# A fused attention and convolution network in fp32: one weight sum per attention block, adding transfers for three of fifteen additions, and compact divisions

## The chip, the cores and the metric

The kernel runs on one core of one Trainium2 chip. The metric is device time in microseconds (us) of one execution. The kernel before took 2679.58 us, the median of three runs (2674.23 to 2680.1). The profile comes from one further execution.

The core has five engines, each with a queue of its own that is worked off in order: TensorE (PE) for matmuls, VectorE (DVE) for elementwise work and reductions, ScalarE (ACT) for activation functions and copies, GpSimd (POOL), and SyncE (SP), which here issues the DMAs. Matmuls write PSUM, which has eight banks of 512 fp32 columns; everything else lives in SBUF.

## The reference

The input is 16 frames of 384 channels and 16 x 16 points, in two batches of 2048 tokens each. Four layers follow each other; all numbers are fp32. The change is in layer 0, attention in 12 heads of 32 channels, whose values are the input itself:

```python
xt = x.reshape(B, NUM_FRAMES, C, H, W).transpose(0, 2, 1, 3, 4)
xt = xt.reshape(B, C, N).transpose(0, 2, 1)
qk = (xt @ qk_w.T).reshape(B, N, 2, nh, HEAD_DIM)
...
attn = jax.nn.softmax(jnp.einsum('bhnd,bhmd->bhnm', q * scale, k), axis=-1)
...
attn = alpha * eye + beta * attn - gamma * Cm
out = jnp.einsum('bhnm,bhmd->bhnd', attn, v)
```

Layer 1 is a 7 x 7 depthwise convolution, a layer norm, a two-matrix MLP with a gelu and a response norm, and a residual. Layer 2 is two Sobel edge maps, a fusion matmul, a layer norm, a gelu and a residual. Layer 3 is two pointwise convolutions with a 3 x 3 depthwise one between them, linear attention, and a second MLP.

## The kernel before, in words

**Blocks.** A batch is cut into four blocks of 512 tokens (`BLK`), so there are eight blocks in the layers behind attention. In attention a *unit* is one batch and one group of four heads (six units); a unit has four blocks of 512 queries, so there are 24 attention *blocks*, and each has 16 *steps* `t`, one for every 128 keys.

**One step.** `scores` runs four matmuls of 32 rows, one for each head, into two double-bank PSUM tiles `st`, and two exps of 128 x 1024 into two SBUF tiles `e` (L461 to L479). The loop (L585 to L595) emits the scores of step t+1 before the `weighted` of step t. `weighted` (L481) runs four matmuls of 32 columns that add the four heads' weighted values into one bank `av`, and then VectorE adds the exps into running sums `s`, two additions of 128 x 1024. An fp32 matmul is recorded as two instructions, so four heads show as eight.

**Weight sums.** The softmax's denominators are sums of the exps over the keys. VectorE adds up `adds` steps' exps elementwise, and TensorE then sums over the 128 partitions by a matmul with ones into the bank `dn` (`weights`, L524). `ADDS` (L55) holds for each of the 24 blocks how many steps go into one sum: 16, 8, 4 or 2. All but a block's last sum are cut into four quarters of 128 columns that are spread over later steps (L505 to L512).

**End of a block.** `finish` (L536) copies `dn` to `r` with a row total for the safety test, and puts four reciprocals of 128 x 128, a scaling of `va` by `r`, the output `put` and a second total `check` into `due`, a table of what is to be emitted at which later step. `va` and `xg` (L516 to L521) are ScalarE's copy of `av` and the part with alpha and gamma.

**Projections.** In step 5 (`SLOT`) of most blocks two projections of the next queries or keys run, three matmuls of 128 x 512 each (L592).

**Filling.** `fill` (L1481) uses VectorE's free time in attention for layer 1's convolutions of the first two blocks (`YB`), written as `y`, and for the first steps of layer 1 itself (the `leads`: a centring with a matmul `su`, a variance with a matmul `sv`, a square root, a reciprocal). `pace` (L194) holds the time that the planner expects of each step on TensorE and VectorE. PSUM in attention is three double tiles for scores and projections, and one bank each for `av` and `dn` (L412, L413).

**Behind attention** everything is written as tasks of operations with costs, and `Plan.all` (L180) emits them in an order that it works out from those costs, from `RANK` and `SLACK`. `TURNS` (L36) is the order in which blocks pass through the two MLPs; at every turn the MLP's weights are loaded anew, three times 768 KB for each of two matrices.

`InOrder` (L96) records every operation, so nearly all rows of the profile have this line and are told apart by their tiles.

Of the kernel before, what the change touches and what calls it, by code (L numbers as in the profile page):

```python
# [13 lines left out]
PSUM = bass.MemoryType.PSUM  # L14

P = 128
# [15 lines left out]
SLOT = 5  # L32
LEAD = 20 * NQC + 6
# [4 lines left out]
    (1, ((0, 0), (0, 1),)),  # L38
    (0, ((1, 0), (1, 2),)),
    (1, ((0, 2),)),  # L40
    (0, ((1, 1), (1, 3),)),
    (1, ((1, 0), (0, 3), (1, 2), (1, 1), (1, 3),)),
)
AFTER = ('x4', 0, 2)

RANK = {
    "mid": ((36.6, 22.0, 24.3, 85.6), (18.6, 42.9, 96.6, 26.9)),
    "l1": ((50.1, 89.5, 75.2, 4.0), (51.1, 16.8, 81.7, 28.5)),
    "l3c": ((45.7, 99.2, 100.9, 121.0), (-20.9, -6.3, 70.9, 62.0)),
    "conv": 109.4,  # L50
}
SLACK = 0.196
JUNK = 2

ADDS = (16, 8, 16, 16, 4, 4, 4, 2, 2, 8, 16, 16, 4, 16, 2, 4, 16, 8, 4, 4, 4, 4, 4, 4)  # L55
# [61 lines left out]
class Plan:  # L117
# [24 lines left out]
    def run(self, op):  # L142
        at = self.start(op)
        assert at is not None
        for tag, n in op.takes:
            del self.room[tag][:n]
        if op.engine == "PE" and at - self.free_at["PE"] > 2:
            at += 1.5
        if op.engine:
            self.free_at[op.engine] = at + op.length  # L150
        op.ready = at + op.length + op.lag
        for tag, n in op.gives:
            self.room[tag] = sorted(self.room[tag] + [op.ready] * n)
        if op.makes:
            self.made[op.makes] = op
        self.table = op.table or self.table
# [37 lines left out]
def pace(t):  # L194


    n, i = divmod(t - 1, NQC)
    adds = ADDS[n]
    pe, dve = 2.066, 2.275 if t and i % adds else 0.0
    at = i - adds - 1  # L200
    parts = sum(j * adds // 4 == at % adds for j in range(4)) if at >= 0 else 0
    if parts:
        pe += 0.22 * parts
    elif i == 1 and n > 0:
        pe += 0.87
    else:
        pe += 0.09
    if n > 0:
        dve += {2: 0.88, 3: 0.88, 4: 0.88, 5: 0.88, 6: 0.6, 7: 0.66}.get(i, 0.0)
    return pe, dve  # L210
# [187 lines left out]
def attention(tc, X, xt, L0, block, small, col, cols, ones, load_qk, banks, fill, bound):  # L398
# [6 lines left out]
    with ExitStack() as actx:  # L405
# [3 lines left out]
        ep = pool("ep", 8)  # L409
        sp = pool("sp", 4)  # L410
        op = pool("op", 2)
        pst = pool("pst", 3, space=PSUM)  # L412
        pacc = pool("pacc", 1, space=PSUM)  # L413

        def bank2(name):
            return pst.tile([P, 2, BLK], F32, tag="st", name=name)

        banks.append(lambda name: bank2(name)[:, 0, :])
# [35 lines left out]
        due = {}  # L454

        def unit(u, made, gm):
# [3 lines left out]
            adds = ADDS[u * NBLK : (u + 1) * NBLK]  # L460
            acc, sums = {}, {}  # L461

            def scores(n, t):
                es = []
                for i in range(2):
                    es.append(ep.tile([P, 2, BLK], F32, tag="e", name=f"e_{u}_{n}_{t}_{i}"))
                sts = [bank2(f"st_{u}_{n}_{t}_{i}") for i in range(2)]
                for h in range(4):
                    rows = slice(HD * h, HD * (h + 1))
                    pe.matmul(  # L470
                        sts[h // 2][:, h % 2, :],
                        keys[t // TB][rows, ts(t % TB, P)],
                        q[n][rows, :],
                        start=True,
                        stop=True,
                    )
                for i in range(2):
                    act.activation(es[i], sts[i], AF.Exp, scale=HD**-0.5)
                return es  # L479

            def weighted(n, t, es):  # L481
                if t == 0:
                    acc["av"] = pacc.tile([P, BLK], F32, tag="av", name=f"av_{u}_{n}")
                for h in range(4):
                    pe.matmul(
                        acc["av"][HD * h : HD * (h + 1), :],
                        v[t // TB][:, (t % TB) * P + HD * h : (t % TB) * P + HD * (h + 1)],
                        es[h // 2][:, h % 2, :],
                        start=(t == 0),
                        stop=(t == NQC - 1),  # L490
                    )
                at = t % adds[n]
                for i in range(2):
                    if at == 0:
                        sums[i] = es[i]
                    elif at == 1:
                        s = sp.tile([P, 2, BLK], F32, tag="s", name=f"s_{u}_{n}_{t}_{i}")
                        dve.tensor_tensor(s, sums[i], es[i], ALU.add)
                        sums[i] = s
                    else:  # L500
                        dve.tensor_tensor(sums[i], sums[i], es[i], ALU.add)


                k = (u * NBLK + n) * NQC + t
                if at == adds[n] - 1:  # L505
                    parts = 1 if t == NQC - 1 else 4
                    for i in range(parts):
                        due.setdefault(k + 2 + i * adds[n] // 4, []).append(
                            lambda i=i, summed=dict(sums): weights(
                                n, t, summed, ts(i, BLK // parts)  # L510
                            )
                        )  # L512
                for f in due.pop(k, ()):
                    f()
                if t == NQC - 1:
                    va = op.tile([P, BLK], F32, tag="va", name=f"va_{u}_{n}")  # L516
                    act.activation(va, acc["av"], AF.Copy, scale=1.0)
                    xg = op.tile([P, BLK], F32, tag="xg", name=f"xg_{u}_{n}")
                    act.activation(
                        xg, X[b][n][:, g, :], AF.Identity, scale=col("alpha", g), bias=gm  # L520
                    )  # L521
                    due[k + 2].append(lambda: finish(n, va, xg))

            def weights(n, t, summed, at):  # L524
                if t == adds[n] - 1 and at.start == 0:
                    acc["dn"] = pacc.tile([P, BLK], F32, tag="dn", name=f"dn_{u}_{n}")
                for h in range(4):
                    pe.matmul(
                        acc["dn"][HD * h : HD * (h + 1), at],
                        ones[:, :HD],  # L530
                        summed[h // 2][:, h % 2, at],
                        start=(t == adds[n] - 1 and at.start == 0),
                        stop=(t == NQC - 1),
                    )

            def finish(n, va, xg):  # L536
# [4 lines left out]
                r = op.tile([P, BLK], F32, tag="r", name=f"r_{u}_{n}")  # L541
                act.activation(r, acc["dn"], AF.Identity, accum_out=bound[:, 0, k : k + 1])

                def invert(i):
                    dve.reciprocal(r[:, ts(i, P)], r[:, ts(i, P)])
# [3 lines left out]

                def check():  # L550
                    junk = op.tile([P, BLK], F32, tag="junk", name=f"junk_{u}_{n}", bufs=1)
                    act.activation(junk, r, AF.Identity, accum_out=bound[:, 1, k : k + 1])
# [6 lines left out]
                todo = [*(lambda i=i: invert(i) for i in range(TB)), scale, put]  # L559
                for i, f in [*enumerate(todo), (8, check)]:  # L560
                    due.setdefault((k + 1) * NQC + 2 + i, []).append(f)
# [7 lines left out]
        def project(name, steps):  # L569
            pp = bank2(name)  # L570
            for copy in [f(pp[:, i, :]) for i, f in enumerate(steps)]:
                copy()
            return 2.7 * len(steps)
# [5 lines left out]
        for u, (b, g) in enumerate(units):  # L579
# [5 lines left out]
            for n in range(NBLK):  # L585
                for t in range(NQC):
# [5 lines left out]
                    if t == SLOT and steps:  # L592
                        added = project(f"p_{u}_{n}", steps[:2])
                        del steps[:2]
# [10 lines left out]
def conv_seq_kernel(  # L605
# [381 lines left out]
    def second(hid, first, name, ready, last, before=None):  # L987

        po = []
        for f in range(NFC):  # L990
# [6 lines left out]
                gives=[("s", 1)] + ([("wb", 1)] if last and f % NG == NG - 1 else []),  # L997
# [14 lines left out]
    def layer1(b, i):  # L1012
# [8 lines left out]
        gx = pools["tiny"].tile([P, 2, NFC], F32, tag="gx", name=f"gx_{n}")  # L1021
# [56 lines left out]
        po, m = yield from second(hid, at, n, None, last, normed)  # L1078
# [342 lines left out]
    def layer3c(b, i):  # L1421
# [11 lines left out]
        po, m = yield from second(hid, at, n, made, last)  # L1433
# [41 lines left out]
    if fast:  # L1475
# [5 lines left out]
        def fill(t, added=0.0):  # L1481
# [3 lines left out]
            if t < 0:  # L1485
                while plan.step(bias):
                    pass
                return
            if t % NQC == 9 and t > NQC:
# [4 lines left out]
            for task in (*leads, conv):  # L1494
                if task.rest > t or t < (FIRST if task is conv else LEAD):
                    continue
                before = None
                while task is not conv or ("y", 0, YB - 1, NC - 1) not in plan.made:
                    op = task.head
                    if before and before.engine != op.engine:  # L1500
                        task.rest = t + 1 + (before.engine == "DVE")
                        break
                    if op.engine == "DVE":
                        if free < max(0.4, op.length - 1.5):
                            break
# [146 lines left out]
```

## Time and profile before

| | |
|---|---|
| runs shown | 2674.23, 2680.1, 2679.58 us; median 2679.58 |
| the profiled execution | 2679.38 us, span 2677.6 us, mean granted TensorE clock 0.996 |
| PE busy | 2644.6 us (99%), 12997 matmul instructions |
| DVE busy | 2011.5 us (75%) |
| ACT busy | 1557.5 us (58%) |
| POOL busy | 7.4 us |
| DMA | 55.69 MB, 21 GB/s in the mean |
| exps (ACT) | 768 of 128 x 1024, 1025 ns each |
| additions of exps (DVE) | 606 of 128 x 1024, 1216 to 1221 ns each |
| weight sums (PE) | 2016 instructions |
| reciprocals of r (DVE) | 96 of 128 x 128, 939 ns each |

The span is the time between the first and the last instruction; the 1.8 us that the execution took longer lie around it. Attention's first scores start at 22.07 us and layer 1's first MLP matmul at 1052.3 us, so there are three stages: a start, attention, and the rest.

How to read the rows: a row of the timeline gives the start in us, the length in us of all its merged instructions, the engine, the line, the operation, out<-in by the tiles' names, the shape, how many were merged, and in brackets the idle time of the engine before it and what ended that. A row of groups gives busy us and mean ns of one, then idle time before them. A matmul's end is modelled, so for TensorE the distances between starts are the better measure. A duration on ScalarE or VectorE overlaps a little with the next one on that engine. A row of DMA issues gives how many, KB each, and the median us from issue to landing.

### The profile page before, as it was taken

Reading aid. Unit: us, or ns where it says so; the run is one execution under the profiler, and the core shown is the slowest. Engines: PE = TensorE matmul, PEld = TensorE weight load, DVE = VectorE, ACT = ScalarE, POOL = GpSimd, SP = SyncE. Lnnn points to the kernel's source line nnn. Section 1 sums busy time; section 2 is a strip of 40 time slices with the busy share of each in tenths; the row PEclk is TensorE's granted clock in tenths of the full one; section 3 lists DMA queues with packets and bytes.
Section 4 is the critical chain, followed back from the end, with each engine's and each line's share of the span. In section 5 each row is a group of like instructions: output and inputs, shape, how many; then the busy total and the mean of one; then the engine's idle time right before and its main releaser. Section 6 shows DMA issues by size and latency. Waiting matters only on the chain. (4 is left out here: it accounts for less than half of the span.)

```text
span 2677.6 us, 32803 instructions
## 1 busy us (share of the span) xinstructions
PE 2644.6 (99%) x12997; PEld 1061.5 (40%) x12997; DVE 2011.5 (75%) x2588; ACT 1557.5 (58%) x2314; POOL 7.4 (0%) x54
## 2 busy tenths in 40 slices
PE   8999999999999999899999999999999999999999
PEld 2223333233323323345444454444444444454443
DVE  5999999999999889999999999999652202732300
ACT  6787878878787888564565335457443542625201
POOL 0000000000000000000000000000000000000000
PEclk9999999999999999999999999999999999999999
DMA  3000000000000003000001001011001110000000
GB/s 150 5 13 1 9 9 5 13 1 5 13 1 1 1 13 108 23 0 0 1 1 47 25 12 31 29 36 36 24 24 36 47 36 24 0 1 1 12 17 20
DMA packets 28851, 55.69 MB, mean 21 GB/s; under 512 B 1680, under 2 KB 14096, under 8 KB 28688
## 3 DMA queue, kind: packets, MB, share of 16 engines
q1 hardware_dynamic: 28544, 53.35, 6.0%
q8 instruction: 104, 1.70, 0.3%
q14 instruction: 59, 0.48, 0.1%
q10 hardware_dynamic: 144, 0.15, 0.0%
HBM read 47.21 MB, written 6.29 MB: 20 GB/s over the span
## 5 line engine op out<-in xcount | busy, mean ns | idle before, releaser
L96 ACT ACTIVATE e<-st 128x1024 f32<-128x1024 f32 x768 | 743.2, 1025 | 88.5 <-PE st L96 80.7
L96 DVE SCALAR_TENSOR_TENSOR y<-l,vec,y 128x420 f32<-128x420 f32 (+8 forms) x1152 | 660.0, 638 | 5.0
L96 DVE TENSOR_TENSOR s<-s,e 128x1024 f32<-128x1024 f32 x444 | 513.3, 1216 | 11.7 <-ACT e L96 11.2
L96 PE MATMUL st<-q,k 32*128 32x512 f32 x3072 | 474.1, 641 | 4.0 <-ACT e L96 2.3
L96 PE MATMUL av<-e,v 128*32 128x512 f32 x3072 | 410.9, 606 | 4.3 <-ACT va L96 4.2
L96 PE MATMUL ph_l<-y,wa 128*128 128x512 f32 x576 | 261.4, 597 | 0.0
L96 PE MATMUL ph_l3c<-d_l3c,wa 128*128 128x512 f32 x576 | 258.4, 593 | 0.0
L96 PE MATMUL po_l<-hid_l,wb 128*128 128x512 f32 x576 | 255.7, 596 | 1.1 <-ACT hid_l L96 1.1
L96 PE MATMUL po_l3c<-hid_l3c,wb 128*128 128x512 f32 x576 | 256.6, 593 | 0.0
L96 PEld LDWEIGHTS st<-q,k 32*128 32x128 f32 x3072 | 146.1, 183 | 220.1 <-issue 132.4
L96 DVE TENSOR_TENSOR s<-e,e 128x1024 f32<-128x1024 f32 x162 | 191.0, 1221 | 54.7 <-ACT e L96 36.0
L96 ACT ACTIVATE hid_l<-ph_l,vec 128x512 f32<-128x512 f32 x96 | 66.0, 687 | 202.9 <-PE ph_l L96 202.8
L96 ACT ACTIVATE hid_l3c<-ph_l3c,vec 128x512 f32<-128x512 f32 x96 | 65.6, 687 | 202.6 <-PE ph_l3c L96 202.5
L96 PEld LDWEIGHTS av<-e,v 128*32 128x32 f32 x3072 | 60.6, 108 | 298.1 <-issue 274.0
L96 DVE SCALAR_TENSOR_TENSOR o_l3c<-po_l3c,vec,l 128x512 f32<-128x512 f32 x24 | 17.5, 748 | 209.6 <-PE po_l3c L96 208.8
L96 PEld LDWEIGHTS po_l<-hid_l,wb 128*128 128x128 f32 x576 | 109.5, 191 | 139.1 <-issue 128.0
L96 PEld LDWEIGHTS ph_l3c<-d_l3c,wa 128*128 128x128 f32 x576 | 108.8, 190 | 137.2 <-issue 133.4
L96 PEld LDWEIGHTS ph_l<-y,wa 128*128 128x128 f32 x576 | 109.1, 191 | 136.0 <-issue 125.1
L96 PEld LDWEIGHTS po_l3c<-hid_l3c,wb 128*128 128x128 f32 x576 | 109.0, 190 | 134.6 <-issue 132.8
L96 PE MATMUL p<-x,wqk_sb 128*128 128x512 f32 x288 | 132.3, 610 | 1.2 <-DMA x<-in_x_dram 1.2
L96 DVE SCALAR_TENSOR_TENSOR g_l3a<-h_l3a,dw,g_l3a 128x450 f32<-128x450 f32 (+1 forms) x192 | 119.0, 702 | 4.2 <-ACT g_l3a L96 4.1
L96 PEld LDWEIGHTS dn<-s,ones 128*32 128x32 f32 x2016 | 64.1, 110 | 125.4 <-issue 107.0
(155 smaller groups left out, 2446.3 us busy)
## 6 DMA issues: line engine op xcount, KB each, us to landing
wa<-in_w_dram SPq DMA_DIRECT2D x9, 768.0 KB, 4.5
wb<-in_w_dram SPq DMA_DIRECT2D x9, 768.0 KB, 5.0
wa<-in_mlp_w_dram SPq DMA_DIRECT2D x9, 768.0 KB, 4.4
wb<-in_mlp_w_dram SPq DMA_DIRECT2D x9, 768.0 KB, 4.5
x<-in_x_dram SPq DMA_DIRECT2D x8, 768.0 KB, 10.6
v<-in_xt_dram SPq DMA_DIRECT2D x24, 256.0 KB, 2.7
out_dram<-o_l3c SPq DMA_DIRECT2D x24, 256.0 KB, 2.1
qkv<-in_qkv_wT_dram SPq DMA_DIRECT2D x3, 576.0 KB, 11.1
```

The lines of the kernel that those rows point to most:

```text
L96: self.last = self.tc.keep_in_program_order(make(*args, **kw))
```

## The change

It touches attention, and the planner around it.

- **Exps.** A step's four heads get one SBUF tile `e` of 4 x 512 (six of them, in place of eight of 2 x 512 and four sums). PSUM is eight single banks, shared by scores, `av`, `dn` and projections; each head has a bank and an exp of 128 x 512 of its own.
- **Additions.** Each block has one weight sum of all 16 steps. The exps of step 2 are the accumulator. Steps 0, 5 and 10 (`MERGED`) receive the exps of the step behind them by a DMA that adds within SBUF, issued by GpSimd, and VectorE adds the three merged tiles at steps 6, 11 and at the block's end; nine more steps are added by VectorE directly.
- **Weight sum.** Four matmuls with ones once a block, emitted behind the next block's first step and its projections (in the last three blocks three steps later).
- **Divisions.** The denominators of a head stand in 32 equal rows. One row for each head goes to DRAM, comes back as 128 x 16, is inverted there, goes to DRAM again, and comes back spread over 32 rows, by seven DMAs on SP.
- **Projections** move from step 5 to step 0.
- **Filling.** Operations of the leads that switch ScalarE's tables are emitted only at a block's start. `LEAD` lets the first lead in from step 294 and the second not within attention. `pace` has new numbers.
- **Behind attention** `TURNS` has eight turns in place of six, and `RANK`, `SLACK` and `AFTER` have new values; `spent` gives a weight buffer back when the last block of a turn has used it; `gx` has four buffers.

```diff
-ADDS = (16, 8, 16, 16, 4, 4, 4, 2, 2, 8, 16, 16, 4, 16, 2, 4, 16, 8, 4, 4, 4, 4, 4, 4)
+MERGED = {0: 6, 5: 11, 10: NQC}
+PAIRED = (NB * NC - 1) * NBLK + 1
+LEAD = (18 * NQC + 6, 24 * NQC)
...
-    (1, ((0, 0), (0, 1),)),
-    (0, ((1, 0), (1, 2),)),
-    (1, ((0, 2),)),
-    (0, ((1, 1), (1, 3),)),
-    (1, ((1, 0), (0, 3), (1, 2), (1, 1), (1, 3),)),
+    (1, ((0, 0),)),
+    (0, ((1, 0),)),
+    (1, ((0, 1),)),
+    (0, ((1, 2),)),
+    (1, ((1, 0),)),
+    (0, ((1, 3), (1, 1),)),
+    (1, ((0, 2), (0, 3), (1, 2), (1, 1), (1, 3),)),
...
-        ep = pool("ep", 8)
-        sp = pool("sp", 4)
+        ep = pool("ep", 6)
         op = pool("op", 2)
-        pst = pool("pst", 3, space=PSUM)
-        pacc = pool("pacc", 1, space=PSUM)
+        pb = pool("pb", 8, space=PSUM, reuse_waits="tile")
+        dp = pool("dp", 2, space=DRAM)
...
-                for i in range(2):
-                    act.activation(es[i], sts[i], AF.Exp, scale=HD**-0.5)
+                for h in range(4):
+                    act.activation(es[:, h, :], sts[h], AF.Exp, scale=HD**-0.5)
...
+                if t in MERGED:
+                    acc[t] = es
+                elif t - 1 in MERGED:
+                    nc.gpsimd.dma_start(acc[t - 1], es, accum_op=ALU.add)
+
+                    def merge(other=acc[t - 1], sums=acc):
+                        dve.tensor_tensor(sums[2], sums[2], other, ALU.add)
+
+                    when = MERGED[t - 1]
+                    if when == NQC and block < PAIRED:
+                        late.append(merge)
                     else:
-                        dve.tensor_tensor(sums[i], sums[i], es[i], ALU.add)
...
+                        due.setdefault(block * NQC + when, []).append(merge)
+                elif t == 2:
+                    acc[2] = es
+                else:
+                    dve.tensor_tensor(acc[2], acc[2], es, ALU.add)
+                if end:
+                    f = lambda summed=acc[2]: weights(n, summed)
+                    if block < PAIRED:
+                        late.append(f)
+                    else:
+                        due.setdefault(k + 3, []).append(f)
...
+                sums = op.tile([P, BLK], F32, tag="sums", name=f"sums_{u}_{n}", bufs=1)
+                act.activation(sums, acc["dn"], AF.Identity, accum_out=bound[:, 0, k : k + 1])
+                away = dp.tile([4, BLK], F32, tag="away", name=f"away_{u}_{n}")
+                nc.sync.dma_start(away, sums[0:P:HD, :])
+                few = op.tile([P, BLK // HD], F32, tag="few", name=f"few_{u}_{n}")
+                nc.sync.dma_start(few, away.rearrange("h (j k) -> (h j) k", j=HD))
+                r = op.tile([P, BLK], F32, tag="r", name=f"r_{u}_{n}", bufs=1)
+
+                def invert():
+                    dve.reciprocal(few, few)
+                    back = dp.tile([P, BLK // HD], F32, tag="back", name=f"back_{u}_{n}")
+                    nc.sync.dma_start(back, few)
+                    for h in range(4):
+                        nc.sync.dma_start(
+                            r[ts(h, HD)],
+                            back[ts(h, HD)]
+                            .rearrange("j k -> (j k)")
+                            .unsqueeze(0)
+                            .to_broadcast([HD, BLK]),
+                        )
...
-                    if t == SLOT and steps:
-                        added = project(f"p_{u}_{n}", steps[:2])
-                        del steps[:2]
+                    if t == 0 and steps:
+                        fill((u * NBLK + n) * NQC, None)
+                        many = 1 if len(steps) == NBLK - 1 else 2
+                        added = project(f"p_{u}_{n}", steps[:many])
+                        del steps[:many]
+                    for f in behind:
+                        f()
+                    behind.clear()
...
+            if added is None:
+                for task in leads:
+                    if task.head.table:
+                        plan.step(task)
+                return
```

## The prediction

> **What bounds the kernel now.** I read the busy shares by stage first, then TensorE's instructions in order of time, then ScalarE's and VectorE's beside them.
>
> The table by stage (us; busy us of PE, PEld, DVE, ACT, POOL; clock; DMA) for start, attention and the rest:
>
> ```profile
> 0.00:22.07 22.07, 16.14 (x32) 7.06 (x32) 3.27 (x19) 3.92 (x7) 0.70 (x6) 1.00 0.93 369
> 22.07:1052.30 1030.23, 1021.90 (x8423) 318.45 (x8422) 962.66 (x1013) 837.38 (x992) 0.00 (x0) 1.00 0.03 8
> 1052.30:2677.60 1625.30, 1606.52 (x4545) 735.98 (x4543) 1045.59 (x1556) 716.17 (x1315) 6.74 (x48) 0.99 0.08 24
> ```
>
> TensorE is busy in both stages; a busy PE can be waiting inside, so I go to single steps. TensorE in order of time (start, length), in a block of 16 additions, then in one with sums every four steps:
>
> ```profile
> 129.11 1.14 PE L96 MATMUL st<-q,k 32*128 32x512 f32 x8
> 130.19 1.07 PE L96 MATMUL av<-e,v 128*32 128x512 f32 x8
> 131.18 1.31 PE L96 MATMUL st<-q,k 32*128 32x512 f32 x8
> 132.42 1.06 PE L96 MATMUL av<-e,v 128*32 128x512 f32 x8
> 133.42 1.14 PE L96 MATMUL st<-q,k 32*128 32x512 f32 x8
> ...
> 202.73 5.42 PE L96 MATMUL p<-x,wqk_sb 128*128 128x512 f32 x12
> 208.07 1.14 PE L96 MATMUL st<-q,k 32*128 32x512 f32 x8
> 209.15 1.06 PE L96 MATMUL av<-e,v 128*32 128x512 f32 x8
> 210.03 0.40 PE L96 MATMUL dn<-s,ones 128*32 128x128 f32 x8
> 210.36 1.14 PE L96 MATMUL st<-q,k 32*128 32x512 f32 x8
> ```
>
> A free step is 2.07 us (129.11 to 131.18): 1.07 for scores, 1.00 for the weighted values. Every second step is 2.24 (131.18 to 133.42): its second pair of scores waits until an exp has freed one of three double PSUM tiles. A quarter of a weight sum costs 0.22 (208.07 to 210.36 is 2.29), a pair of projections 5.34 (202.73 to 208.07). So attention is TensorE's time plus small waits. That the other engines have room:
>
> ```profile
> 211.53 1.94 ACT L96 ACTIVATE e<-st 128x1024 f32<-128x1024 f32 x2 [0.34 <-PE st L96]
> ...
> 208.18 1.07 ACT L96 COPY q<-p 128x512 f32<-128x512 f32 x2 [4.35 <-PE p L96]
> ...
> 133.48 14.85 DVE L96 TENSOR_TENSOR s<-s,e 128x1024 f32<-128x1024 f32 x13
> ```
>
> ScalarE does a step's exps in 1.94 and then idles; VectorE, without a wait, adds 1024 columns every 1.14 us.
>
> **The sum of attention before.** 384 steps x 2.07 = 795. Projections: 259 recorded matmuls / 6 = 43 x 2.67 = 115. Weight sums: 1824 / 8 = 228 quarters x 0.22 = 50, and 192 / 8 = 24 last ones of 512 columns, each 1.02 (step of 3.09 in the blocks after finely summed ones, less 2.07) = 24. Two matmuls of layer 1: 2. That is 986; the remaining 44 of 1030 are waits, 1.8 a block.
>
> **The change part by part.**
>
> *One weight sum a block.* The built order of the changed kernel has 96 weight-sum matmuls where there were 1008. The 228 quarters go: **-50 us**, all on TensorE, which sets the end. The last sum now stands behind a pair of projections (5.34). VectorE's last two additions (2 x 2.3) follow the exps of step 15 and end about 1.1 + 4.6 = 5.7 after the next block's first step begins, TensorE arrives at 2.07 + 5.34 = 7.4; hidden with 1.7 us to spare. In the last three blocks there are no projections and the sum comes three steps later, which covers it too. At the very end nothing covers it: some 5 us, as now.
>
> *Single banks and exps of 512.* Eight single banks replace three pairs and two: with one bank held by av, a step's scores wait for the exp of the step before only at the fourth head. The 0.17 of every second step goes where nothing else took it. Most blocks with quarters hide it already, so I do not count it by blocks but in the waits below. Price: 768 exps become 1536. Two copies of 512 from PSUM stand 0.48 apart (1.07 less one duration of 0.59), so four exps take 1.93 against 2.07 for TensorE. Bounds: 4 x 0.48 (no loss) and 4 x 0.61, the mean of a lone 512 PSUM read (va, 608 ns) = 2.43, +0.36 a step, +138 us. I take 0.48, since the exps queue back to back as those copies do. The Trainium skill, "ScalarE: Activation LUTs", section "Rules for kernel authors", speaks against the split: it budgets about 0.3 us per activation (with a bias as pointer) plus 0.83 ns an element, which as an estimate makes four exps 2.9 us and attention 319 us longer. The pair of copies above against the pair of exps (0.48 for 512, 0.92 for 1024) leaves 0.04 fixed, so I follow the rows.
>
> *Adding transfers.* 288 additions of 2048 columns replace 606 of 1024; at 2 x 1.14 each that is 657 against 691 us of VectorE: hidden either way. What matters is the landing: the source's buffer is one of six, and in the built order the exps of steps 6, 10 and 15 wait for a transfer. It can be issued when its source's exps end, 1.17 + 2.03 = 3.2 after that step begins; the exp that takes the buffer wants to start 1.17 after its own step begins, five steps later for the first (8.3 us allowed), four for the others (4 x 2.07 + 1.17 - 3.2 = **6.25 us** allowed). GpSimd holds nothing but these transfers, so nothing queues behind them; ScalarE's next exps do, and TensorE waits for those. No row shows an adding transfer or one within SBUF. Plain loads:
>
> ```profile
> wa<-in_w_dram SPq DMA_DIRECT2D x9, 768.0 KB, 4.5
> ...
> v<-in_xt_dram SPq DMA_DIRECT2D x24, 256.0 KB, 2.7
> ```
>
> give 1.8 fixed + 3.6 per MB: 5.4 for 1 MB copied, 9.0 if the second operand doubles the traffic. I take 6.7, nearer the plain rows because neither end is in HBM: 2 x 0.45 = 0.9 a block, **+22 us**. Ends: 0, and (2 x 2.75 + 0.7) x 24 = +149. The skill's "DMA: Bandwidth & Descriptors", section "Anatomy of one DMA", fits 2.0 us plus bytes at 436 GB/s, 4.4 for 1 MB and, as an estimate, 6.8 for twice the traffic; no run here shows it, and it would make +26.
>
> *Compact divisions.* 4 x 0.94 of RECIPROCAL a block become one of 16 columns (0.17 by the small ones): -85 us of VectorE, hidden now, worth nothing itself; it lets the planner move the 33 missing convolution taps of the first two blocks into attention (289 y instructions instead of 256). Instead SP carries seven small transfers: four landings in series. At 2.1 to 2.7 each (out 2.1, v 2.7) they take 8.4 to 10.8; the sums are ready 0.9 into step 1, VectorE reaches the scaling 13.4 after step 1 began (exps of step 4 end at 9.4, an addition of 2.3, three taps of 0.57): 1.7 spare. If late, VectorE's next merge and the buffers behind it are late as well; SP's v loads queue behind them but are due blocks later. I cost it at nothing.
>
> *Waits left.* Some 7 of the 44 are one place: at 972 TensorE idles 0.83 and 1.21 us behind ScalarE's square root of layer 1 with its table loads (1.28 each), and the granted clock in 975 to 985 is 0.70. The changed planner lets an operation that switches tables go only at a block's start, beside the projections; that goes. So do the 2.24 steps. What stays: start 3, end 5, 0.5 a block where va and xg delay the exps = 12: 20 of the 44. **-24 us.**
>
> *Behind attention* the same matrices and a new order. TensorE has one real hole there:
>
> ```profile
> 1089.16 1.10 PE L96 MATMUL su_l<-s_l,ones 128*128 128x512 f32 x2 [3.65 <-DVE s_l L96]
> 1092.19 0.59 PE L96 MATMUL pg_l<-gs_l,ones 128*128 128x2 f32 x2 [1.93 <-DVE gs_l L96]
> 1094.90 2.05 PE L96 MATMUL sv_l<-s_l,ones 128*128 128x512 f32 x2 [2.13 <-DVE gmean_l L96]
> ```
>
> 7.7 us idle, and the granted clock in 1090 to 1100 is 0.51. With the second block's convolution done inside attention, its su stands six matmuls into the stage instead of 36: **-10 us** (7.7 and part of the slow clock). Two more weight turns reload 4.5 MB each behind 10 us of matmuls per load of 4.5 us: nothing. Bounds of the new order: -15 to +15.
>
> **Sum.** The profiled execution took 2679.4 (span 2677.6 + 1.8), practically the median 2679.58. 2679.4 - 50 - 24 + 22 - 10 = **2617 us**.
>
> **Rivals.**
> 1. *The transfer lands in time* (at most 6.25 us): 2595. For: DMA is busy 3% of attention, so it runs alone. Against: a second operand. 25%.
> 2. *Transfer about 7.2*: 2 x 0.95 x 24 = +46, 2641; or exps at 0.54 apart (4 x 0.54 = 2.16, +35), likewise about 2650: half the gain goes to a new wait. 15%.
> 3. *Slower: adding transfers run at half rate.* The gain without any transfer wait is 84 us; 24 x 2 x (D - 6.25) eats it at D = 8.0 us. At 9.0 it is 2595 + 149 = 2744, and more if each 2.75 us hole halves the clock as the one above did. For: two operands read per element written; against: idle engines. 19%.
> 4. *Nothing measurable*: D between 7.9 and 8.1, or a post-attention order that gives all back. 5%.
> 5. *The change does not do what it says*: the built order has the 96, 288 and 1536 instructions, so only its waits are open.
>
> **Chances.** The forecast (2605 to 2635) has 36%. 0.2%, 5 us, is about what a measurement of this kernel can tell from no change: faster 0.76, same 0.05, slower 0.19. The range for 8 in 10 reaches from 2588 (first rival with a good order) to 2690; beyond it lies most of the third.
>
> **What would show it.** Right: free steps of 2.07 without the 2.24; eight-matmul sums 24 times; exps of 512 about 0.48 apart; attention ending near 985; landing of e<-e under 7 us. Wrong: ScalarE idle before the exps of steps 10 and 15 with a DMA as releaser; VectorE idle before the scaling; clock under 1 inside attention. The weakest number is the transfer's 6.7 us.

## The result, and the profile after

The changed kernel takes **2711.7 us** (median of 4 runs, 2707.0 to 2714.0) against 2679.6 for the kernel before in the same session: ratio 1.0129, 95% interval 1.0116 to 1.0143. Forecast was 2617, 2588 to 2690; it is 95 us above the forecast and slower than before. The profiled execution has a span of 2710.2 us, 32.6 more than before.

The table by stage, as in the prediction (stretch; length; busy us of PE, PEld, DVE, ACT, POOL; clock; DMA share; GB/s):

```profile
21.60:1071.10 1049.50, 1029.78 (x6599) 277.75 (x6598) 877.83 (x659) 876.33 (x1760) 62.06 (x72) 0.99 0.41 86
1071.10:2710.20 1639.10, 1608.28 (x4547) 738.60 (x4543) 1020.34 (x1520) 742.16 (x1337) 6.76 (x48) 0.99 0.09 30
```

Attention did not fall from 1030 to 978, it rose to 1049.5; the rest did not fall from 1625 to 1615, it rose to 1639.1. TensorE's work did go: the weight sums are 192 matmuls of 512 columns now. So waits have taken its place. ScalarE in order of time (start, length, count, idle before and its releaser) in the block from 114 to 158:

```profile
125.43 8.39 ACT L100 ACTIVATE e<-st 128x512 f32<-128x512 f32 x16
136.28 4.03 ACT L100 ACTIVATE e<-st 128x512 f32<-128x512 f32 x8 [2.46 <-DMA e<-e]
```

and GpSimd and TensorE beside it:

```profile
127.79 0.86 POOL L498 DMA_DIRECT2D e<-e  x1 [9.82 <-ACT e L100]
```

```profile
134.85 1.13 PE L100 MATMUL st<-q,k 32*128 32x512 f32 x6
136.93 1.12 PE L100 MATMUL st<-q,k 32*128 32x512 f32 x2 [0.95 <-ACT e L100]
...
150.70 5.42 PE L100 MATMUL p<-x,wqk_sb 128*128 128x512 f32 x12
```

The 16 exps from 125.43 are steps 6 to 9. Step 6 is the source of the block's second transfer: its exps end at 127.5, GpSimd issues at 127.79. Step 10's first exp takes that buffer; ScalarE is free for it at 133.8, 6.0 after the issue, and starts at 136.28, 8.5 after it, released by the transfer. TensorE finds no free PSUM bank after six matmuls of the next scores. This step, the eleventh, lasts 3.0 to 4.8 us in most blocks, and a block 43.5 in the mean, where the forecast's 978 makes 40.8. The DMA issues (count, KB each, median us from issue to landing):

```profile
e<-e POOLq DMA_DIRECT2D x72, 1024.0 KB, 7.2
...
v<-in_xt_dram SPq DMA_DIRECT2D x24, 256.0 KB, 10.7
```

The transfer takes 7.2 in the median, 6.9 to 9.6 in all; 6.25 were allowed. The waits of attention (us in total, times, longest):

```profile
ACT e L100 <- DMA e<-e: 58.3, 43, 3.4
...
DVE few L100 <- DMA few<-away: 23.9, 13, 6.8
DVE va L100 <- DMA r<-back: 23.4, 20, 2.9
```

And the end of attention, VectorE first, then TensorE:

```profile
1059.82 9.41 DVE L100 TENSOR_TENSOR e<-e,e 128x2048 f32<-128x2048 f32 x4
1077.84 0.25 DVE L100 RECIPROCAL few<-few 128x16 f32<-128x16 f32 x1 [8.61 <-DMA few<-away]
1084.69 0.69 DVE L100 TENSOR_TENSOR va<-va,r 128x512 f32<-128x512 f32 x1 [6.60 <-DMA r<-back]
```

```profile
1071.15 7.53 PE L100 MATMUL ph_l<-y,wa 128*128 128x512 f32 x12
1087.62 2.08 PE L100 MATMUL su_l<-s_l,ones 128*128 128x512 f32 x2 [8.95 <-DVE s_l L100]
```

Nothing covers the last block's chain of small transfers, and in SP's queue it stands between weight loads of 768 KB. VectorE's first sum for layer 1 (s_l, over y) stands behind the scaling in its queue, so TensorE waits 8.95 for it: the old hole of 3.65 at this matrix product has come back larger, for another reason. The product that follows runs at half clock (two matmuls in 2.08; the same two take 1.10 before).

### The profile page after: what moved, and what is told of

Same layout as the page of the kernel before. It is cut to its first block, busy times and chain, and to the rows that moved or that the text cites. A ratio compares the mean times of both kernels' runs of the same rounds, so it can differ in the third digit from the quotient of the medians.

```text
span 2710.2 us, 29416 instructions
## 1 busy us (share of the span) xinstructions
PE 2653.5 (98%) x11173; PEld 1023.2 (38%) x11173; DVE 1901.4 (70%) x2198; ACT 1622.6 (60%) x3104; POOL 69.5 (3%) x126
## 4 chain that ended last, share of the span: by engine, by line
PE 84%; DVE 6%; DMA 5%; issue 3%; ACT 2%; SPq 0%; ACTq 0%; DVEq 0%; POOLq 0%
PE st L100 13%; PE av L100 12%; PE po_l L100 9%; PE ph_l3c L100 9%; PE po_l3c L100 9%; PE ph_l L100 6%; PE p L100 5%; DMA e<-e 4%; PE pf_l L100 4%; PE pk_l3b L100 2%; PE pv_l3b L100 2%; PE pd_l3a L100 2%; PE pq_l3b L100 2%; DVE y L100 2%; PE pp_l3b L100 2%
## 5 line engine op out<-in xcount | busy, mean ns | idle before, releaser
L100 ACT ACTIVATE e<-st 128x512 f32<-128x512 f32 x1536 | 788.8, 618 | 99.3 <-DMA e<-e 58.3
L100 DVE TENSOR_TENSOR e<-e,e 128x2048 f32<-128x2048 f32 x288 | 659.6, 2290 | 127.4 <-ACT e L100 58.2
L100 PE MATMUL st<-q,k 32*128 32x512 f32 x3072 | 480.7, 644 | 14.4 <-ACT e L100 11.5
L100 PE MATMUL av<-e,v 128*32 128x512 f32 x3072 | 458.8, 609 | 0.0
L100 PEld LDWEIGHTS st<-q,k 32*128 32x128 f32 x3072 | 138.1, 184 | 360.1 <-issue 288.9
L100 PEld LDWEIGHTS av<-e,v 128*32 128x32 f32 x3072 | 87.1, 108 | 314.2 <-issue 275.4
L100 ACT ACTIVATE hid_l<-hid_l,vec,gx_l 128x256 f32<-128x256 f32 x192 | 103.1, 616 | 3.4 <-DVE gx_l L100 3.4
## 6 DMA issues: line engine op xcount, KB each, us to landing
v<-in_xt_dram SPq DMA_DIRECT2D x24, 256.0 KB, 10.7
```

Source lines behind the costliest of these rows:

```text
L100: self.last = self.tc.keep_in_program_order(make(*args, **kw))
```

## The experiments

Four theories of the loss. **A**: the adding transfers land later than the exps that take their buffers can wait. **B**: exps in parts of 512 saturate ScalarE. **C**: the small transfers of the divisions hold VectorE. **D**: the new order behind attention costs the 14 us there. "Before" in each ratio is the kernel before on the same chip.

**e1: no adding transfers, VectorE adds all sixteen tiles**

```diff
-MERGED = {0: 6, 5: 11, 10: NQC}
+MERGED = {}
...
-                elif t == 2:
+                elif t == 0:
                     acc[2] = es
```

(and 2.35 of VectorE for each of 15 steps in the planner's pace)

> The changed kernel, but VectorE makes all 15 additions of a block and no transfer adds. Theory A (the adding transfers land 7.0 to 9.6 us after they are issued where 6.25 is allowed, and ScalarE's exps of steps 10 and 15 wait for them): ScalarE's 58 us of idle time behind e<-e go, the long eleventh step (3.0 to 4.8 us) goes, attention shortens from 1049 to about 995 us and the time falls to about 2655 us. Theory B (the exps in four parts keep ScalarE busy at 2.12 us a step): steps stay at 2.12 and the time stays within 10 us of 2712. Theory C (the seven small DMAs of a division hold VectorE): within 10 us of 2712 too. VectorE has 15 x 2.2 = 33 us of additions in blocks of about 41 us, so some taps of the convolution may move behind attention.

2790.0, ratio 1.0425 (1.0407 to 1.0442). A block takes 41.0 and the long step is gone, as A says. But VectorE, with 15 additions a block, is busy 911 of the 979 us up to the last step's scores and has then issued only 104 of the 289 y instructions of the first two blocks' convolutions. TensorE pays for it after the last block:

```profile
1037.19 4.00 PE L100 MATMUL pb<-sh_L_bn__92,ca 128*128 128x1 f32 x18 [22.71 <-DMA ca<-in_cw1T_dram]
1117.81 2.07 PE L100 MATMUL su_l<-s_l,ones 128*128 128x512 f32 x2 [76.62 <-DVE s_l L100]
```

(The first wait ends when the load of `ca` lands, at 1037.1: this product needs no y and stands first in TensorE's queue there. The second, longer one is for y.) What the transfers buy is VectorE's time.

**e2: whole reciprocals, no small transfers**

```diff
-                    dve.reciprocal(few, few)
+                    dve.reciprocal(r[:, ts(i, P)], r[:, ts(i, P)])
```

(four of these a block, on the sums as copied from PSUM; the seven transfers go)

> The changed kernel with the four reciprocals of 128 x 128 of the kernel before, and without the seven small DMAs. Theory C: transfers no longer share the DMA engines with the small ones and land after 7.0 us throughout, VectorE no longer waits (24 us for few, 23 us for r), and at attention's end the chain few, back, r no longer leaves TensorE idle 9 us at 1078: 30 to 40 us faster, about 2675. Theory A: the long eleventh step shrinks from 3.0-4.8 to about 2.9 but stays, 10 to 20 us faster, plus the hole at the end, about 2690. Theory B: no change in attention, only the hole at the end, about 2700. VectorE gets 3.3 us more a block.

2759.0, ratio 1.0306 (1.0289 to 1.0323). The long step stays at 3.0 to 5.5, so C is not its cause. The v loads land in 4.6 instead of 10.7, so it is the small transfers ahead of them that make these late; nothing waits for them. Behind attention TensorE idles 18.5, 6.1, 4.6 and 8.3 us between 1060 and 1106: the planner, told of 3.35 us more of VectorE a block, put only 212 of the 289 y instructions ahead of the last weight sum. Without the compact divisions the kernel loses 47 us. VectorE was busy 885 of the 1028 us up to the last scores, so this run prices the divisions together with what the planner makes of them; it does not show that VectorE had no room.

**e3: the order of before behind attention**

```diff
-AFTER = ('x4', 0, 1)
+AFTER = ('x4', 0, 2)
-SLACK = 0.381
+SLACK = 0.196
```

(and TURNS and RANK of before)

> The changed kernel with the order behind attention of the kernel before (TURNS, AFTER, RANK, SLACK, six turns). Theory D (the new order costs the 14 us that the stage behind attention is longer): the stage falls from 1639 to 1625 us, time about 2698. Theories A and C: the stage stays at 1635 to 1645 because the hole at 1078 comes from the division chain and not from the order, time about 2710.

2829.7, ratio 1.0578 (1.0561 to 1.0596); the rest takes 1756.8 instead of 1639.1. D is not confirmed. These constants suit only the kernel that they were found for, so this run does not tell what the order by itself is worth.

**e4: double PSUM tiles and exps of 1024, all else changed**

```diff
-                for h in range(4):
-                    act.activation(es[:, h, :], sts[h], AF.Exp, scale=HD**-0.5)
+                for i in range(2):
+                    act.activation(es[:, 2 * i : 2 * i + 2, :], sts[i], AF.Exp, scale=HD**-0.5)
```

> The changed kernel with the PSUM layout of the kernel before: three double tiles and two single banks, two exps of 128 x 1024 a step. Theory B: ScalarE has room again (1.94 a step) and catches up after each wait; 15 to 25 us faster, about 2690. Theory A: the waits for the transfers stay, steps go to the pattern 2.07 and 2.24 (2.155 in the mean instead of 2.125); 0 to 15 us slower, 2712 to 2727.

2710.9, ratio 1.0127 (1.0111 to 1.0144), attention 1050.5: no difference. B falls as the cause of the loss. Steps are 2.07 and 2.24 here, 2.07 and 2.18 in the changed kernel; the long step is in both.

**e5, e6, e7: transfers of half the size; whole reciprocals in the last three blocks; both**

```diff
-                    nc.gpsimd.dma_start(acc[t - 1], es, accum_op=ALU.add)
+                    nc.gpsimd.dma_start(acc[t - 1][:, :2, :], es[:, :2, :], accum_op=ALU.add)
+                    dve.tensor_tensor(
+                        acc[t - 1][:, 2:, :], acc[t - 1][:, 2:, :], es[:, 2:, :], ALU.add
+                    )
```

```diff
+                if k >= PAIRED:
+                    few = r
+                    act.activation(r, acc["dn"], AF.Identity, accum_out=bound[:, 0, k : k + 1])
...
+                        for i in range(TB):
+                            dve.reciprocal(r[:, ts(i, P)], r[:, ts(i, P)])
```

> The changed kernel, but each adding transfer carries heads 0 and 1 only (512 KB); VectorE adds the other 1024 columns to the same accumulator (72 more additions of 1.14 us, 82 us of VectorE, told to the planner as 1.2 each). Theory A (the 1 MB transfers land 7.0 to 9.6 us after issue where 6.25 are allowed, and the late exp holds TensorE): half the bytes land in about 5 us, within the allowance; the step of 3.0 to 4.8 us in each block goes back to about 2.1, a block takes 41 instead of 43.6, attention about 990 to 1000 instead of 1049.5, the kernel about 2655, unless VectorE's 82 us push layer 1 out of attention (then a hole of TensorE appears behind attention, as in the run without transfers). Rival: the long step comes from the exps' pace or the small transfers, not from the adding transfer: then the long steps stay and the kernel takes 2710 or more.

> The changed kernel, but the last three blocks, which have no projections, divide by four whole reciprocals of 128x128 without the small transfers (12 more reciprocals of 0.94, 11 us of VectorE). Theory C restricted to the end of attention (the chain of small transfers holds VectorE, which then reaches the next blocks' merges and layer 1's squares late): the steps of 5.45 and 6.37 go (8 us), the wait of TensorE for layer 1's square behind attention (8.95 us) and the half clock after it go or shrink (10 to 15 us): 2690 or a little under. If that hole is made by something else, 2700 to 2712.

> Both edits: half-size adding transfers, and whole reciprocals in the last three blocks. If A and C both hold and add up, 2630 to 2645, under both kernels; if VectorE has no room for the 82 us of additions, 2680 to 2720 with TensorE waiting behind attention.

e5: 2743.6, ratio 1.0245 (1.0228 to 1.0262). Half the bytes land in 4.6:

```profile
e<-e POOLq DMA_DIRECT2D x72, 512.0 KB, 4.6
```

The eleventh step goes back to 2.2 and a block to 41.9: A's mechanism is shown a second time. The total is a miss: told of 82 us more for VectorE, the planner put 213 of the 289 y instructions ahead of the last weight sum, though VectorE was busy only 891 of the 998 us up to the last scores; TensorE waits 22 and 11 us behind it, at a clock of 0.53 over 65. e6: 2694.4, ratio 1.0069 (1.0051 to 1.0087), 17 us under the changed kernel and close to its expectation. Attention is 7.8 shorter, the rest 11.7, and the wait for layer 1's s_l is gone:

```profile
1064.51 3.39 DVE L100 RECIPROCAL r<-r 128x128 f32<-128x128 f32 x4 [2.27 <-ACT r L100]
1067.93 0.69 DVE L100 TENSOR_TENSOR va<-va,r 128x512 f32<-128x512 f32 x1
```

```profile
1070.79 1.13 PE L100 MATMUL su_l<-s_l,ones 128*128 128x512 f32 x2 [0.43 <-DVE s_l L100]
```

Four reciprocals take 3.39 where the chain of transfers took from 1071.8 to 1084.7. So C holds at the end of attention, where nothing covers it, and the 14 us behind attention are mostly this. e7: 2739.1, ratio 1.0227 (1.0210 to 1.0244): e5's hole again, its expectation of 2630 to 2645 missed for the same reason.

**e8: the kernel before with one weight sum a block and nothing else**

```diff
-ADDS = (16, 8, 16, 16, 4, 4, 4, 2, 2, 8, 16, 16, 4, 16, 2, 4, 16, 8, 4, 4, 4, 4, 4, 4)
+ADDS = (16,) * 24
```

> The kernel before, with one weight sum a block throughout (16 additions everywhere, all on VectorE, double PSUM tiles, four whole reciprocals): the first part of the change alone. The 228 quarter sums leave TensorE (50 us), but VectorE gets 24 x 15 additions of 2.3 us = 828 us and 90 us of reciprocals in 985 us, so the taps of layer 1's convolution don't fit. Theory (VectorE is the second bound and the finer sums were the price for its time): attention about 990, and behind it a hole of 50 us and more with a slow clock: 2700 to 2790. Rival (VectorE is hidden, as the prediction had it): 2630 to 2650.

2814.4, ratio 1.0510 (1.0493 to 1.0528). The two stretches up to the last step's scores and from there to layer 1's first product:

```profile
22.20:1008.00 985.80, 978.35 (x6563) 273.12 (x6562) 949.79 (x906) 821.10 (x974) 0.00 (x0) 1.00 0.03 8
1008.00:1168.80 160.80, 15.74 (x59) 6.27 (x55) 153.91 (x236) 13.42 (x21) 0.00 (x0) 0.52 0.16 54
```

The first is 38 us shorter than before (last scores at 1046.51, less 22.07, is 1024.4): most of the 50 that the prediction counted. VectorE then works 154 of 161 us while TensorE works 16, at a clock of 0.52. Up to there it had issued 51 of the 256 y instructions that the kernel before has done in attention, at 950 us busy of 986. VectorE is the second bound: the finer weight sums of before paid TensorE's time for VectorE's.

**f1, f2: the transfer issued as two of 512 KB; the same with whole reciprocals in the last three blocks**

```diff
-                    nc.gpsimd.dma_start(acc[t - 1], es, accum_op=ALU.add)
+                    for h in (0, 2):
+                        nc.gpsimd.dma_start(
+                            acc[t - 1][:, h : h + 2, :], es[:, h : h + 2, :], accum_op=ALU.add
+                        )
```

> The changed kernel, but each adding transfer is issued as two of 512 KB, heads 0 and 1 and heads 2 and 3; the first can go when the exps of its two heads have ended, about 1 us before the whole one could. Same bytes, same work of VectorE. Measured so far: 6.1 us from the end of issue to landing for 1 MB, 3.7 for 512 KB. Theory A: the first lands about 3.7 after an issue that ends 1 us earlier, the second about 4.6 to 5.5 after the exps, within the 6.25 allowed and not at 7.0 and later; the step of 3.0 to 4.8 goes from most blocks, a block takes 42 instead of 43.6, attention 1005 to 1020 instead of 1049.5, the kernel 2665 to 2680 (the wait behind attention stays, since the divisions are those of the changed kernel). Rival: the bytes set the landing and the two share the queue, so nothing lands earlier: 2705 to 2715.

> The pieces of the first run of this call, and whole reciprocals in the last three blocks as in the run that gave 2694. If both causes are independent, the gain of the pieces (30 to 40 us, by theory A) and that of the last divisions (16) add: 2645 to 2665, under both kernels. If the pieces bring nothing, 2690 to 2697.

f1: 2678.0, ratio 1.0003 (0.9992 to 1.0014), attention 1014.2. The bytes are the same, and so is the work of the engines but for GpSimd's second issue. The first half is issued 0.6 us before the last exp of its source ends, and the whole of a block's second transfer lands 7.3 behind that end in the median, where it was 7.9. With that 35 us of attention are back: the rival (same landing) is out. f2: 2663.9, ratio 0.9954 (0.9937 to 0.9970): both gains add, and the kernel is faster than before. ScalarE still waits 27.2 us for the transfers in it, 28 times.

**g1: the adding transfers left out, nothing in their place**

```diff
-                    nc.gpsimd.dma_start(acc[t - 1], es, accum_op=ALU.add)
```

> The changed kernel with the 72 adding transfers left out and nothing in their place: three of the sixteen tiles of each block are missing from its weight sums, all else is as it was. What the transfers cost by being late is then the whole difference. Theory A: ScalarE never waits for a transfer, the long step goes (2.1), a block takes about 41.2: attention 995 to 1005, that is 45 to 55 us less than the changed kernel's 1049.5, and the kernel 2655 to 2665. If the remaining 2.07 and 2.18 in turn came from the transfers too, steps go to 2.07 and attention to 985. If the loss is elsewhere, 2700 or more.

This kernel leaves three of the sixteen tiles out of every sum, so it is a price and not a version. 2646.8, ratio 0.9882 (0.9865 to 0.9898):

```profile
21.50:1005.70 984.20, 976.51 (x6599) 261.88 (x6598) 875.51 (x659) 878.35 (x1760) 0.00 (x0) 1.00 0.05 15
```

Attention is 65.3 us shorter at the same work of VectorE and ScalarE, and the rest unchanged (1639.5): **the transfers cost 65 us**, and the runs before this one show that they do so by landing late. Attention came out 11 under its expectation of 995 to 1005, so A's share had been put too low. The steps stay at 2.07 and 2.19; that is not the transfers.

**g2: f2 with head 3 added by VectorE**

```diff
-                    for h in (0, 2):
+                    for h in (slice(0, 2), slice(2, 3)):
...
+                    dve.tensor_tensor(acc[t - 1][:, 3, :], acc[t - 1][:, 3, :], es[:, 3, :], ALU.add)
```

(and 0.2 in the planner's pace for each, which leaves as many y instructions in attention)

> The version that gave 2663.9 (two pieces, whole reciprocals at the end), but the transfers carry heads 0 and 1 and then head 2, and VectorE adds head 3 (72 additions of 512 columns, about 0.6 us each, 43 us), while the planner is told of only 0.2 each, so that as many taps of layer 1 as before go into attention. Theory A: 25% fewer bytes and an earlier landing take what is left of the wait at the eleventh step (about 0.9 a block): attention 990 to 1000 and the kernel 2640 to 2655, if VectorE, at 920 busy of some 1000, still keeps up. If VectorE is the bound there, its additions come late, the exps wait for them and not for the transfer, and the kernel takes 2665 to 2700.

2648.8, ratio **0.9887** (0.9870 to 0.9903), the best complete version:

```profile
21.10:1020.50 999.40, 982.83 (x6599) 263.25 (x6598) 923.52 (x737) 879.17 (x1760) 126.19 (x144) 0.99 0.37 71
```

```profile
ACT e L100 <- DMA e<-e: 6.0, 9, 1.3
```

VectorE is busy 924 of 999 us and still keeps up; ScalarE waits 6 us for transfers where it waited 58.

## Why the prediction was wrong, step by step

The forecast's attention was 1030 - 50 - 24 + 22 = 978; measured 1049.5. Its rest was 1625.3 - 10 = 1615; measured 1639.1. The 95 us are 71.5 and 24.

1. **The transfer's 6.7 us, the step that failed most.** It lay between the plain rows' 5.4 and 9.0 for twice the traffic, put low because "neither end is in HBM". Measured: 7.2 in the median for 1 MB and 4.6 for 512 KB, that is 2.0 fixed and 5.2 per MB. (The Trainium skill's estimate that the prediction set beside it, "DMA: Bandwidth & Descriptors", section "Anatomy of one DMA" with twice the traffic, 6.8, was nearer than the value taken.) The term was +22; g1 measures **+65**. At 7.2 the prediction's own formula gives 24 x 2 x 0.95 = 46. But its allowance of 6.25 counts from the end of the source's exps, and GpSimd issues 0.29 behind that. Counted so, a block's second transfer lands after 7.9 in the median and the third after 7.3, and the formula gives 24 x (1.63 + 1.08) = 65. That it meets the 65 so closely is in part luck: taken transfer by transfer, with the spread, it gives 75. By place, the distances between the scores are 36 us longer than in g1 at the eleventh step, 20 at the first step of a block and 9 elsewhere. The second rival had named a landing of 7.2 and priced it at the same 46. The slower rival had the right place and sign, but not the rate: 9.0 for 1 MB was not reached. It put its turning point at 8.0, since it had 84 us of gain to eat. Without transfers the kernel gains 33 (2679.4 to 2646.8), so by the same formula that point was at 6.25 + 33/48 = 6.9.
2. **One weight sum, -50: about right.** The eight-matmul sums are there once a block, and e8's steps are 38 shorter with some waits longer.
3. **Exps of 512 at 0.48 apart: right, but the 2.24 steps did not go.** ScalarE and TensorE in g1, where no transfer is waited for:

```profile
111.70 10.57 ACT L100 ACTIVATE e<-st 128x512 f32<-128x512 f32 x20 [0.33 <-PE st L100]
```

```profile
112.61 1.14 PE L100 MATMUL st<-q,k 32*128 32x512 f32 x8
113.68 1.18 PE L100 MATMUL av<-e,v 128*32 128x512 f32 x8
114.80 1.14 PE L100 MATMUL st<-q,k 32*128 32x512 f32 x8
115.87 1.06 PE L100 MATMUL av<-e,v 128*32 128x512 f32 x8
```

Inside a step the exps stand 0.48 to 0.49 apart. 20 in 10.57 are 0.53 each, since the first of the next step comes 0.62 or more after the last, and in 340 of 383 steps the trace names the scores as what released it. In turn, in every second step the last of the weighted matmuls waits for the fourth exp: the group lasts 1.18 instead of 1.06, one matmul of it starts at 113.82 and the exp ends at 113.77. Steps are 2.07 and 2.18 in turn, 2.125 in the mean, and 384 x 0.055 = 21 us stay that had been let go with "the 2.24 steps". The second rival's 0.54 apart and +35 came near for ScalarE's mean, but not by the pace of its exps: with whole exps of 1024, e4 has steps of 2.07 and 2.24.
4. **Waits left, 20: too low.** g1's attention is 984.2, the work that the prediction's sum leaves 936 (986 less 50): 48 of waits. With each step's own work taken off the distances between the scores, 19 of the 24 blocks wait 0.9 to 1.8 us, 25 in all, most of it the 21 of point 3. The last block waits 8.4, of which 4.3 is for its weight sum, as foreseen; four others wait 2.7 to 5.3. The place at 972 shrank: the block in which g1 loads the square root's tables (847 to 852) waits 5.3, some 4 more than most, at a clock of 1.00. Of the 71.5 in attention, 43 are thus the transfers (65 for 22) and 28 the waits left (48 for 20).
5. **Compact divisions at nothing: right inside, wrong at the end.** Inside attention VectorE waits for r (23.4 us in all), but e2, without these transfers, has the same long steps. The chain took longer than the 8.4 to 10.8 assumed: `back` took 6.3 in the median from issue to landing beside the adding transfers, 1.4 in g1. At the end of attention the chain has no cover, and e6 prices that at 17 us. "Hidden now, worth nothing itself" holds only together with the y instructions that the planner moves for it (e2).
6. **Behind attention, -10: wrong sign.** +14 was measured; 12 of the 24 us between are the last division (e6: 1627.4). The hole at su is gone in e6, as predicted, and still the rest is 2 above before. Other holes have come (in e6 2.54 at 1107 and 3.66 at 1198). What the new order alone is worth was not separated; it stays open.
7. **VectorE taken as hidden.** The prediction saw it busy 963 of 1030 and gave it no price. In e1 and e8 it is nearly full (911 of 979, 950 of 986), and the convolutions that did not fit come back as idle time of TensorE behind attention. In e2 and e5 the same idle time comes although VectorE had room, because the planner was told of more work; g2, which told it of less, adds 40 us to f2's VectorE (924 of 999) and loses nothing. That bears less on the 95 us, since the changed kernel balances it, than on why the change needs its transfers at all.

What would show it wrong had been named rightly: ScalarE idle before a block's eleventh step with a DMA as releaser, and a clock under 1 inside attention (0.66 from 835 to 845, behind a wait of 2.82 us).

## What to carry to other kernels

A transfer that takes work from an engine sets a date for the buffer it reads; price it from a measured one (7.2 us for 1 MB added, where the rows of loads made 5.4), count it from the end of the work that fills the source, compare with the steps until that buffer is written again, and issue it in pieces as its source becomes ready: the same bytes in two pieces turned a loss of 1.3% into none. An engine that is over 90% busy beside the bound one is not hidden but nearly the next bound: 72 more additions of 2.3 us (e1) came back as a wait of 77 us behind the stage, while 40 us more (g2) still fitted. A chain of latencies that is free in the middle of a pipeline is paid in full in its last blocks, so those may need the other form.

## What the runs showed of the hardware

- An adding transfer within SBUF: 7.0 (e2) to 7.2 us for 1 MB, 4.6 for 512 KB in the median, of which GpSimd's issue is 0.86. Two of 512 KB one behind the other (f1): 4.6 to 4.8 for the first, 6.3 to 7.0 for the second, 6.1 in the median of all. Single ones took up to 9.6; what makes these longer was not found (without the small transfers, in e2, some still take over 8).
- TensorE's clock: a wait of 8.95 us was followed by matmuls at half speed, and while TensorE was busy 15.74 of 160.8 us the granted clock was 0.52. "TensorE: Matmul & The Clock Gate" of the skill says, in its Part 1, that an idle window of about 3.4 us drops the clock to half; these two rows agree. The stretch at 975 to 985 of the kernel before does not: there two waits of 0.83 and 1.21 came with a clock of 0.70, so less than such a window was enough. Nor does a single wait of 2.82 in the changed kernel, with 0.66 from 835 to 845. One of 1.43 in g1, at 849, left the clock at 1.00.
- Loads of 256 KB on SP's queue took 2.7 us before, 10.7 behind the small transfers (also in g1, without adding transfers) and 4.6 in e2, beside adding transfers alone.
- A store of 8 KB on SP's queue (`back`) took 6.3 us from issue to landing in the median beside the adding transfers and 1.4 without them (g1). In the block shown it was issued at 118.13 and landed at 124.28, 0.16 behind the adding transfer that had been issued at 117.11.
